# A graph attention kernel: candidate lists by quarters, and two VectorE products moved to ScalarE

## The chip, the cores and the metric

The kernel runs on one core of a Trainium2 chip. A core has five engines with a queue each, worked off in order: TensorE (PE in the profile, with its weight loads as PEld), VectorE (DVE), ScalarE (ACT), GpSimd (POOL) and SyncE (SP). They share an on-chip memory of 128 partitions (SBUF), an accumulator memory that TensorE writes (PSUM), and 16 DMA engines. The metric is the device time of one execution, from the first to the last instruction with what lies around it. A difference below 0.2% can't be told from none here.

## The reference

Two layers over one adjacency matrix `adj` of 3327 x 3327, of which about 2% of the entries are not zero (some 64 a row, and the diagonal). Layer 0 is graph attention with four heads, layer 1 a normalised graph convolution:

```python
h = jnp.maximum(_layernorm(x, axis=-1), 0.0)
# per head:
x1 = h @ w1;  x2 = h @ w2
E = jax.nn.leaky_relu(x1[:, None, :] + x2[None, :, :], negative_slope=0.01)
s = jnp.tanh((E @ a) / 8.0) * 8.0
s = jnp.exp(s) * adj
s = s / jnp.sum(s, axis=-1, keepdims=True)
out = leaky_relu(s @ h @ Wlin.T, 0.01)
x = x + jnp.concatenate(heads, axis=-1) @ w
# layer 1
h = jnp.maximum(_layernorm(x, axis=-1), 0.0)
A_t = adj + eye(n);  D_inv = A_t.sum(axis=1) ** -0.5
x = x + relu((D_inv[:, None] * A_t * D_inv[None, :]) @ (h @ W.T + b))
```

Only the entries of `adj` that are not zero matter to the scores. The kernel finds them, fetches the rows that they name, and computes the scores of those pairs alone.

## The kernel before

The nodes are padded to 3328 and worked in 26 blocks of 128 rows, each block in two halves of 64 rows. Each node has a row of 776 numbers in a table in device memory (its features, its scores' share, its four projected vectors, and its column of the adjacency matrix for one block); the tables of even and odd blocks alternate.

**Preparation of a block (`prep`).** It is a generator: it yields between small steps, and the steps of the blocks to come are put between the work of the current one. It does the following, in order:

- It turns the 128 x 3328 rows of `adj` into codes, a number for each column that is not zero (L410, L416, L418).
- It searches the codes for the entries: each row is cut into 64 segments of 52 columns, and one `max` (L422) writes the eight largest codes of a segment into `cand`. There the eight ranks of 32 segments lie together. Four ranks are kept as they are; the other four ranks of a half of the row are boiled down to a list of eight (L425).
- Between these searches it transposes the block on TensorE (L365), copies it out on ScalarE (L367) and stores it to device memory through ScalarE's DMA queue (L370). `known_step` uses the same copies for sums of layer 1 (L379, L385).
- ScalarE sums the rows (L443), and `load` fetches the rows of the next block through SP.
- `select` (L453, L456) takes the entries out of the candidates, eight a round, in 13 rounds: a `max` and a `match_replace` that strikes out what was found. The first four rounds go over one half of the candidates each (136 values), in turns; the other nine go over all (272). The first eight rounds give 64 slots a row; the last five give up to 40 further entries a row, the extra edges.
- `lq` spreads the 64 slots (L463, a product with the mask `modsel` on VectorE), TensorE turns them into another order (L470), and L473 makes the row numbers `idx` for the gathers.
- The extra edges of all rows are packed into lists of at most 256 a half block (L481 to L546), and the vectors of the block's own rows are projected (L551 to L568).

**Gathers.** GpSimd fetches the named rows with indirect DMAs of 128 rows each (L595): for a half block 32 of them into `g`, in four groups (w = 0 to 3) of eight, and two for the extra edges into `ge`. `g` has four buffers, `ge` has one. A group's buffer comes free when the last matrix product that reads it (L706 for `g`, L724 for `ge`) has been issued and done.

**Scores (`stage_z`, `stage_r`, `finish`).** For a part of a group, TensorE transposes the gathered vectors into `z` (L622, L625, L627; two buffers in PSUM), VectorE takes the maximum with minus the own vector (L638; L633, and ScalarE's L635, for the extra edges), and TensorE multiplies with the vector a (L657). `finish` closes a group: ScalarE copies the scores out (`ssb`, L666), TensorE transposes them (L675), VectorE adds the rows' shares (L678, L681), ScalarE takes tanh and exp (L686, L688), VectorE multiplies the weights with the adjacency entries (`wt`, L697), and TensorE sums the rows (L706). For the extra edges `am` picks an entry (L713) and `wo` is its product with the four heads' weights (L715), three tiles a half block, and L724 sums. `close` ends a block (L735 to L797).

**What sets the order.** The order is written by hand. `slot` is called 108 times a block, at fixed places between TensorE's instructions; in each it takes one step of every open `close` and `finish`, then as many steps of the preparations as are due (72 a block), then it issues gathers for which a buffer has been given back, and table loads (`weights`, on SP). A yield in `prep` or `finish` thus puts the rest one step later. Each engine then works its queue off in this order, and waits where what it needs isn't there.

**Layer 1** runs at the end (`layer1`): strips of the transposed matrix come in through SP's and ScalarE's DMA queues (L898) into the same `g` buffers, and TensorE multiplies (L988). Part of its sums is made earlier (`begin`, L924).

Last, a check of the lists: if a row had an entry that no list holds, a dense path would run in place of the result.

Of the kernel before, what the change touches and what calls it, by code (L numbers as in the profile page):

```python
# [9 lines left out]
F32 = mybir.dt.float32  # L10
AF = mybir.ActivationFunctionType
OP = mybir.AluOpType
# [3 lines left out]
P = 128  # L16
SLOPE = 0.01
CAP = 8.0
# [213 lines left out]
def _sparse_layers(tc, nc, x, adj, w1, w2, a, wlin, w, gw, gb, gb_sb, gwT, x_sb, dinv, flag, ident, out):  # L232
# [14 lines left out]
    H = w1.shape[0]  # L247
# [5 lines left out]
    WT = 8  # L253
# [3 lines left out]
    with ExitStack() as l0:  # L257
# [19 lines left out]
        modsel = res.tile([P, P], F32, name="modsel")  # L277
# [8 lines left out]
        pb = l0.enter_context(tc.tile_pool(name="pb", bufs=2))  # L286
# [66 lines left out]
        def prep(b, k):  # L353
# [38 lines left out]
                known[:] = [f for f in known if next(f, "end") != "end"]  # L392


            SOME = 8 + 4 * 32
            cand = pb.tile([P, 2, SOME + 4 * 32], F32, name="cand", bufs=1)
            tab_at = 0
            while b == 0 and tab_at < NB:
                tables_step(tab_at)
# [5 lines left out]
            for sgm in range(64):  # L405
                if sgm % 32 == 0:
                    codes = pa.tile([P, 2, part], mybir.dt.uint16, name="codes")
                    for i in range(2):
                        c0 = (sgm // 16 + i) * part
                        nc.vector.scalar_tensor_tensor(codes[:, i], adjb[:, c0:c0 + part], 0.0, code[:, c0:c0 + part],  # L410
                                                       op0=OP.not_equal, op1=OP.mult, accum_out=csum[:, sgm // 16 + i:sgm // 16 + i + 1])
                        lo, hi = max(c0, b * P), min(c0 + part, (b + 1) * P)
                        if lo < hi:
                            diag = pb.tile([P, P], F32, name="lq", bufs=1)[:, :hi - lo]
                            mine = codes[:, i, lo - c0:hi - c0]
                            nc.vector.scalar_tensor_tensor(diag, mine, -1.0, ident[:, lo - b * P:hi - b * P], op0=OP.mult, op1=OP.mult,  # L416
                                                           accum_out=csum[:, sums[0]:sums[0] + 1])
                            nc.vector.tensor_tensor(mine, mine, diag, OP.add)  # L418
                            sums[0] += 1
                        yield  # L420
                c = sgm // 32
                nc.vector.max(cand[:, c, 8:].rearrange("p (r s) -> p r s", s=32)[:, :, sgm % 32],  # L422
                              codes.rearrange("p a b -> p (a b)")[:, sgm % 32 * SEG:(sgm % 32 + 1) * SEG])
                if sgm % 32 == 31:
                    nc.vector.max(cand[:, c, :8], cand[:, c, SOME:])  # L425
                if sgm % 4 == 3:
                    yield
                    known_on()
                if sgm % 8 == 5 and tab_at < NB:
                    tables_step(tab_at)  # L430
                    tab_at += 4
# [14 lines left out]
            lists = pb.tile([P, 64 + 51], F32, name="lists")  # L446
            k.lists = lists
            flat = cand[:, :, :SOME]

            def select(r):  # L450
                top = lists[:, 8 * r:8 * r + 8]
                of = cand[:, r % 2, :SOME] if r < 4 else flat
                nc.vector.max(top, of)  # L453
                yield
                if 8 * r + 8 < 2 * SLOTS + EXTRA:
                    nc.vector.match_replace(out=of, in_to_replace=top, in_values=of, imm_value=0.0)  # L456
                yield

            for r in range(SLOTS // 4):
                yield from select(r)  # L460

            lq = pb.tile([P, 4, 8, 16], F32, name="lq", bufs=1)
            nc.vector.tensor_tensor(lq, modsel.rearrange("p (q s) -> p q s", q=8)[:, None].to_broadcast([P, 4, 8, 16]),  # L463
                                    lists[:, :64].rearrange("p (c s) -> p c s", c=4)[:, :, None, :].to_broadcast([P, 4, 8, 16]), OP.mult)
            yield
            yield
            yield
            pm = bank()
            for c in range(4):
# [191 lines left out]
        def finish(k, hb, w):  # L661
            g, s = k.g.pop((hb, w)), k.s
# [19 lines left out]
                                 k.ex[:, OVT * hb:OVT * hb + OVT, 42:42 + H])  # L682
            yield
            yield
            th = pb.tile([P, WT, H], F32, name="th")
            nc.scalar.activation(th[:, :nt], sc[:, :nt], AF.Tanh, scale=1.0 / CAP)  # L686
            pe = pb.tile([P, WT, H], F32, name="pe")
            nc.scalar.activation(pe[:, :nt], th[:, :nt], AF.Exp, scale=CAP)  # L688
            yield
            yield  # L690

# [20 lines left out]
            for t in range(OVT):  # L712
                nc.vector.scalar_tensor_tensor(am[:, t, :], code[:, :HALF], k.ex[:, OVT * hb + t, 41:42], g[:, t, BODY * hb:BODY * hb + HALF],  # L713
                                               op0=OP.is_equal, op1=OP.mult)
                nc.vector.tensor_tensor(wo[:, t], pe[:, t, None, :, None].to_broadcast([P, 8, H, 8]),  # L715
                                        am[:, t].rearrange("p (g q) -> p g q", q=8)[:, :, None, :].to_broadcast([P, 8, H, 8]), OP.mult)
                yield
            yield
            yield
# [83 lines left out]
        for b in range(NB):  # L803
            k = Blk()
            k.f0 = FEAT, 0
            k.g, k.b, k.ready, k.turned, k.closed = {}, b, False, False, False
            blks.append(k)
        NCODE = 20
        NLIST = 42
        NPREP = 72  # L810
# [553 lines left out]
```

## Time and profile before

| | |
|---|---|
| median of 6 runs | 2501.72 us (2496.91 to 2506.87) |
| the profiled execution | 2504.95 us, its span 2503.2 us |
| mean granted TensorE clock | 0.976 of full speed |
| DMA | 826.94 MB, 330 GB/s over the span; queue of the gathers 70.6% of the 16 engines' span, SP's 18.4%, ScalarE's 7.5% |
| first and last gather issued | 69.7 and 2375.3 us |
| 900 to 1200 us | busy: PE 277.6, DVE 265.6, ACT 84.9, POOL 225.7 us of 300; DMA share 0.99 |
| costliest groups | gathers L595 1614.0 us on POOL; L638 1010.0 us on DVE; L622 933.9 us on PE |
| segment searches L422 | 217.1 us, 1664 of 204 ns |

Times in the timelines are us from the span's start. In a timeline line the first number is the start, the second the length, then engine, line of the code, operation, what is written and read, how many instructions are taken together, and in brackets how long the engine stood idle before it and what ended that. In a line of the groups the count is followed by the busy time in us and the mean of one in ns, then by the idle time before. In a line of the waits the numbers are the sum in us, the number of waits and the longest. In the table by stretch each engine's busy time in the stretch is followed by its number of instructions, then the granted clock of TensorE, the DMA engines' busy share and the rate. A wait is put down to what released it last.

### The profile page before, as it was taken

To read this page: it belongs to the slowest core of one execution; us is meant where nothing else is said; L and a number is where in the kernel's file an instruction comes from. 1 tells how busy PE (TensorE), PEld (TensorE's weight loads), DVE (VectorE), ACT (ScalarE), POOL (GpSimd) and SP (SyncE) were. 2 spreads that over 40 slices of the span, in tenths; PEclk is the share of its full clock that TensorE was granted. 3 is DMA by queue.
4 is the path that set the end of the run, shared out by engine and by line. 5 is a ranking of instruction groups with operands and counts; after the bars stand their busy time and mean duration, and the time that the engine had idled before them with its cause. 6 is when DMAs were issued, how large, how long until landed. Compare 5 with 4: busy or idle time off the path is not lost.

```text
span 2503.2 us, 52385 instructions
## 1 busy us (share of the span) xinstructions
PE 2256.7 (90%) x19410; PEld 1595.7 (64%) x19410; DVE 2063.9 (82%) x6426; ACT 681.8 (27%) x1703; POOL 1737.0 (69%) x1822
## 2 busy tenths in 40 slices
PE   6589989999988998999999999999999999999978
PEld 4466666666666666666666666666676666666643
DVE  7588988888898889889888888988988898896623
ACT  4122232223223222322322232232232223222100
POOL 3477777777777777777777777777777777777700
PEclk8799999999999999999999999999999999999989
DMA  9999999999999999999999999999999999999985
GB/s 290 380 350 330 349 330 321 351 350 313 331 365 330 318 351 350 319 333 358 330 321 348 341 316 334 346 314 334 353 327 322 347 350 317 329 331 350 362 263 160
DMA packets 417844, 826.94 MB, mean 330 GB/s; under 512 B 38435, under 2 KB 288815, under 8 KB 414255
## 3 DMA queue, kind: packets, MB, share of 16 engines
q0 software_dynamic: 141440, 619.41, 70.6%
q1 hardware_dynamic: 165343, 147.87, 18.4%
q10 hardware_dynamic: 110800, 56.25, 7.5%
q8 instruction: 156, 2.56, 0.4%
q14 instruction: 105, 0.86, 0.1%
HBM read 754.47 MB, written 113.22 MB: 347 GB/s over the span
## 4 chain that ended last, share of the span: by engine, by line
PE 37%; DVE 25%; DMA 19%; POOL 11%; issue 6%; ACT 1%; SPq 0%; DVEq 0%; ACTq 0%; POOLq 0%
DMA g<-table,idx 14%; DVE r L638 14%; PE z L622 12%; POOL g L595 11%; PE s L657 10%; DVE cand L422 3%; PE ag L706 2%; PE z L627 2%; DMA g<-AT_d 2%; DVE codes L410 1%; DVE cand L456 1%; PE z L988 1%; DVE lists L453 1%; PE tr L924 1%; PE tr L675 1%
## 5 line engine op out<-in xcount | busy, mean ns | idle before, releaser
L595 POOL DMA_INDIRECT g<-table,idx x1664 | 1614.0, 970 | 586.0 <-issue 420.2
L638 DVE TENSOR_TENSOR r<-z,x1n 128x1024 f32<-128x1024 f32 x832 | 1010.0, 1214 | 129.8 <-PE z L622 127.1
L622 PE MATMUL z<-ident,g 128*128 128x128 f32 x6656 | 933.9, 279 | 102.0 <-DVE r L638 88.3
L622 PEld LDWEIGHTS z<-ident,g 128*128 128x128 f32 x6656 | 754.6, 143 | 263.7 <-DVE r L638 136.8
L657 PE MATMUL s<-r,sel 128*2 128x512 f32 (+1 forms) x3744 | 497.4, 585 | 8.8 <-DVE r L638 4.0
L666 ACT COPY ssb<-s 128x512 f32<-128x512 f32 x260 | 146.8, 565 | 499.6 <-PE s L657 498.8
L657 PEld LDWEIGHTS s<-r,sel 128*2 128x2 f32 x3744 | 79.9, 84 | 250.9 <-issue 188.8
L422 DVE MAX8 cand<-codes 128x8 f32<-128x52 uint16 x1664 | 217.1, 204 | 0.0
L686 ACT ACTIVATE th<-sc 128x32 f32<-128x32 f32 x260 | 58.4, 225 | 438.9 <-DVE sc L681 413.1
L706 PEld LDWEIGHTS ag<-g,wt 128*32 128x32 f32 x3328 | 99.3, 110 | 89.8 <-issue 79.9
L367 ACT COPY at<-tr 128x512 f32<-128x512 f32 (+1 forms) x175 | 97.2, 556 | 212.6 <-PE tr L365 190.8
L675 PE MATMUL tr<-ident,ssb 128*128 128x128 f32 x988 | 150.8, 273 | 2.8 <-ACT ssb L666 2.7
L633 DVE TENSOR_TENSOR r<-z,x1n 128x128 f32<-128x128 f32 x104 | 30.0, 289 | 138.6 <-PE z L627 136.0
L706 PE MATMUL ag<-g,wt 128*32 128x133 f32 x3328 | 140.3, 281 | 0.0
L453 DVE MAX8 lists<-cand 128x8 f32<-128x272 f32 (+1 forms) x338 | 133.2, 394 | 2.2
L365 PE MATMUL tr<-ident,adjb 128*128 128x128 f32 x676 | 109.2, 285 | 24.8 <-DMA adjb<-in_adj_dram 13.0
L635 ACT ACTIVATE r<-z 128x512 f32<-128x512 f32 x104 | 62.2, 598 | 247.2 <-DVE r L633 241.1
L627 PE MATMUL z<-oi,x1b 128*128 128x256 f32 x416 | 125.1, 383 | 0.0
L675 PEld LDWEIGHTS tr<-ident,ssb 128*128 128x128 f32 x988 | 118.1, 141 | 9.7 <-ACT ssb L666 3.4
L595 POOL DMA_INDIRECT ge<-table,idxo x104 | 99.9, 960 | 32.5 <-issue 15.1
L456 DVE MATCH_REPLACE8 cand<-lists,cand 128x272 f32<-128x272 f32 (+1 forms) x312 | 118.0, 378 | 0.0
L410 DVE SCALAR_TENSOR_TENSOR codes<-adjb,code 128x832 uint16<-128x832 f32 x104 | 105.3, 1015 | 13.6 <-DMA adjb<-in_adj_dram 13.6
(199 smaller groups left out, 2410.0 us busy)
## 6 DMA issues: line engine op xcount, KB each, us to landing
adjb<-in_adj_dram SPq DMA_DIRECT2D x26, 1664.0 KB
table<-AT_d SPq DMA_DIRECT2D x26, 1664.0 KB
AT_d<-at ACTq DMA_DIRECT2D x150, 256.0 KB
g<-table,idx POOLq DMA_INDIRECT x1664
table<-img SPq DMA_DIRECT2D x12, 1296.0 KB
adjb<-AT_d SPq DMA_DIRECT2D x72, 128.0 KB
g<-AT_d ACTq DMA_DIRECT2D x25, 256.0 KB
g<-AT_d SPq DMA_DIRECT2D x25, 256.0 KB
```

The costliest lines, as they stand in the source:

```text
L410: nc.vector.scalar_tensor_tensor(codes[:, i], adjb[:, c0:c0 + part], 0.0, code[:, c0:c0 + part], op0=OP.not_equal, op1=OP.mult, accum_out= ...
L422: nc.vector.max(cand[:, c, 8:].rearrange("p (r s) -> p r s", s=32)[:, :, sgm % 32], codes.rearrange("p a b -> p (a b)")[:, sgm % 32 * SEG: ...
L453: nc.vector.max(top, of)
L456: nc.vector.match_replace(out=of, in_to_replace=top, in_values=of, imm_value=0.0)
L595: return nc.gpsimd.indirect_dma_start(out=g[:, t, lo:hi], out_offset=None, in_=tab, in_offset=bass.IndirectOffsetOnAxis(ap=at[:, t:t + 1], ...
L622: nc.tensor.matmul(z[:, i, q * P:(q + 1) * P], g[:, m % 2 * 4 + q, c0:c0 + D], ident, is_transpose=True, start=(q == 0 or m < 8), stop=(m ...
L627: nc.tensor.matmul(z[:, i, :n], k.x1b[:, h * D:(h + 1) * D], k.oi[:, hb * n:(hb + 1) * n], start=False, stop=True, skip_group_check=True)
L638: nc.vector.tensor_tensor(r.rearrange("p h (i s) -> p h i s", s=16), z.rearrange("p h (i s) -> p h i s", s=16), k.x1n[:, 2 * hp:2 * hp + 2 ...
L657: nc.tensor.matmul(k.s[32 * h:32 * h + 2, :n], sel[:, h, 31 - at:33 - at], r[h // 2][:, h % 2, :n], start=(at == 0), stop=(at == 1 or m == 8))
L666: nc.scalar.copy(ssb[:, :nk * P], s[:, :nk * P])
L675: nc.tensor.transpose(pt[:, q, :], ssb[:, q * P:(q + 1) * P], ident)
L706: nc.tensor.matmul(ag[32 * cg:32 * cg + 32, u, :WORK], wt[:, t].rearrange("p h q -> p (h q)"), g[:, t, f0:f0 + WORK], start=(w == 0 and t ...
```

## The change

- The candidates are kept by quarters of the row (16 segments each) in place of halves: three ranks of each segment as they are, and a list of eight from the other five ranks of the quarter (80 values). Two quarters side by side hold 112 candidates, all four 224.
- Of the 13 rounds of `select` the first six, in place of four, go over one half of the row.
- `lq` is made by eight ScalarE activations (a copy with a factor for each row), four in a step and four in the next, in place of one VectorE product. The number of steps stays the same.
- `wo` is made by four ScalarE activations a tile, one for each head, in place of one VectorE product.
- tanh writes over its input; the tile `th` is gone.

```diff
--- before.py
+++ after.py
@@ -392,8 +392,8 @@
                 known[:] = [f for f in known if next(f, "end") != "end"]
 
 
-            SOME = 8 + 4 * 32
-            cand = pb.tile([P, 2, SOME + 4 * 32], F32, name="cand", bufs=1)
+            SOME = 8 + RANKS * 16
+            cand = pb.tile([P, 4, 8 + 8 * 16], F32, name="cand", bufs=1)
             tab_at = 0
             while b == 0 and tab_at < NB:
                 tables_step(tab_at)
@@ -418,10 +418,10 @@
                             nc.vector.tensor_tensor(mine, mine, diag, OP.add)
                             sums[0] += 1
                         yield
-                c = sgm // 32
-                nc.vector.max(cand[:, c, 8:].rearrange("p (r s) -> p r s", s=32)[:, :, sgm % 32],
+                c = sgm // 16
+                nc.vector.max(cand[:, c, 8:].rearrange("p (r s) -> p r s", s=16)[:, :, sgm % 16],
                               codes.rearrange("p a b -> p (a b)")[:, sgm % 32 * SEG:(sgm % 32 + 1) * SEG])
-                if sgm % 32 == 31:
+                if sgm % 16 == 15:
                     nc.vector.max(cand[:, c, :8], cand[:, c, SOME:])
                 if sgm % 4 == 3:
                     yield
@@ -449,7 +449,7 @@
 
             def select(r):
                 top = lists[:, 8 * r:8 * r + 8]
-                of = cand[:, r % 2, :SOME] if r < 4 else flat
+                of = cand[:, r % 2 * 2:r % 2 * 2 + 2, :SOME] if r < 6 else flat
                 nc.vector.max(top, of)
                 yield
                 if 8 * r + 8 < 2 * SLOTS + EXTRA:
@@ -460,10 +460,10 @@
                 yield from select(r)
 
             lq = pb.tile([P, 4, 8, 16], F32, name="lq", bufs=1)
-            nc.vector.tensor_tensor(lq, modsel.rearrange("p (q s) -> p q s", q=8)[:, None].to_broadcast([P, 4, 8, 16]),
-                                    lists[:, :64].rearrange("p (c s) -> p c s", c=4)[:, :, None, :].to_broadcast([P, 4, 8, 16]), OP.mult)
-            yield
-            yield
+            for q in range(8):
+                nc.scalar.activation(lq[:, :, q], lists[:, :64].rearrange("p (c s) -> p c s", c=4), AF.Copy, scale=modsel[:, 16 * q:16 * q + 1])
+                if q % 4 == 3:
+                    yield
             yield
             pm = bank()
             for c in range(4):
@@ -682,10 +682,9 @@
                                  k.ex[:, OVT * hb:OVT * hb + OVT, 42:42 + H])
             yield
             yield
-            th = pb.tile([P, WT, H], F32, name="th")
-            nc.scalar.activation(th[:, :nt], sc[:, :nt], AF.Tanh, scale=1.0 / CAP)
+            nc.scalar.activation(sc[:, :nt], sc[:, :nt], AF.Tanh, scale=1.0 / CAP)
             pe = pb.tile([P, WT, H], F32, name="pe")
-            nc.scalar.activation(pe[:, :nt], th[:, :nt], AF.Exp, scale=CAP)
+            nc.scalar.activation(pe[:, :nt], sc[:, :nt], AF.Exp, scale=CAP)
             yield
             yield
 
@@ -712,8 +711,8 @@
             for t in range(OVT):
                 nc.vector.scalar_tensor_tensor(am[:, t, :], code[:, :HALF], k.ex[:, OVT * hb + t, 41:42], g[:, t, BODY * hb:BODY * hb + HALF],
                                                op0=OP.is_equal, op1=OP.mult)
-                nc.vector.tensor_tensor(wo[:, t], pe[:, t, None, :, None].to_broadcast([P, 8, H, 8]),
-                                        am[:, t].rearrange("p (g q) -> p g q", q=8)[:, :, None, :].to_broadcast([P, 8, H, 8]), OP.mult)
+                for h in range(H):
+                    nc.scalar.activation(wo[:, t, :, h], am[:, t].rearrange("p (g q) -> p g q", q=8), AF.Copy, scale=pe[:, t, h:h + 1])
                 yield
             yield
             yield
@@ -805,6 +804,7 @@
             k.f0 = FEAT, 0
             k.g, k.b, k.ready, k.turned, k.closed = {}, b, False, False, False
             blks.append(k)
+        RANKS = 3
         NCODE = 20
         NLIST = 42
         NPREP = 72
```

## The prediction

> **What bounds the kernel now.** The page's first part comes first: no engine is full, and four resources lie close together. So the next view is busy time by stretch, here over one block (one block is 128 rows, 26 in all) in the middle of the run.
>
> ```profile
> PE 2256.7 (90%) x19410; PEld 1595.7 (64%) x19410; DVE 2063.9 (82%) x6426; ACT 681.8 (27%) x1703; POOL 1737.0 (69%) x1822
> ```
>
> ```profile
> core 0: us, PE busy (x) PEld busy (x) DVE busy (x) ACT busy (x) POOL busy (x), PEclk, DMA share, GB/s
> 1231.00:1265.00 34.00, 31.24 (x285) 22.65 (x284) 30.42 (x83) 9.12 (x21) 25.55 (x27) 1.00 1.02 375
> 1265.00:1297.00 32.00, 30.91 (x280) 22.11 (x278) 24.76 (x70) 9.79 (x30) 24.63 (x25) 1.00 0.93 295
> 1297.00:1320.00 23.00, 20.10 (x178) 14.39 (x177) 22.12 (x90) 6.59 (x16) 15.78 (x17) 0.93 1.00 326
> ```
>
> In the last stretch VectorE is busy 22.12 of 23 us and TensorE is not; in the middle one it is TensorE (30.91 of 32). The DMA engines are full in the outer two. POOL's 25.55 of 34 hides that it hardly pauses by choice: its timeline shows a gather of 0.95 us and a standing pause of 0.30, one after the other.
>
> ```profile
> 1316.47 0.94 POOL L595 DMA_INDIRECT ge<-table,idxo  x1 [0.30 <-PE z L622]
> 1319.80 0.94 POOL L595 DMA_INDIRECT g<-table,idx  x1 [2.39 <-PE ag L706]
> 1321.05 0.94 POOL L595 DMA_INDIRECT g<-table,idx  x1 [0.30 <-issue]
> ```
>
> A block has 68 gathers, so POOL alone needs 68 x 1.25 = 85.1 us. The same gather of the block before starts at 1231.24, so this block took 88.56. The rest is mainly one wait, always at the first gather of a block, for TensorE to be through with a buffer (L706). The waits of POOL between 264 and 2205 us (22 blocks) give its sum:
>
> ```profile
> POOL g L595 <- PE ag L706: 38.2, 25, 3.2
> ```
>
> Less 0.30 of standing pause each, 25 waits hold 38.2 - 7.5 = 30.7 us, 1.23 apiece. So POOL and the consumers (TensorE and VectorE in turns) run at almost one pace, the consumers slower by about 1.4 us a block. A faster consumer can win those 30.7 us in the steady part before POOL binds alone; a slower one costs one for one.
>
> **The change, part by part.** The durations, by shape:
>
> ```profile
> L453 DVE MAX8 lists<-cand 128x8 f32<-128x272 f32 x234 | 102.7, 439 | 2.2
> L456 DVE MATCH_REPLACE8 cand<-lists,cand 128x272 f32<-128x272 f32 x208 | 88.5, 426 | 0.0
> L715 DVE TENSOR_TENSOR wo<-pe,am 128x256 f32<-128x256 f32 x156 | 67.0, 430 | 9.0
> L453 DVE MAX8 lists<-cand 128x8 f32<-128x136 f32 x104 | 30.5, 293 | 0.0
> L456 DVE MATCH_REPLACE8 cand<-lists,cand 128x136 f32<-128x136 f32 x104 | 29.5, 283 | 0.0
> L456 DVE MATCH_VALUE_LOAD cand<-lists,cand 128x8 f32 x312 | 27.3, 88 | 5.6
> L463 DVE TENSOR_TENSOR lq<-modsel,lists 128x512 f32<-128x512 f32 x26 | 17.8, 684 | 0.0
> L425 DVE MAX8 cand<-cand 128x8 f32<-128x128 f32 x52 | 15.4, 295 | 1.8
> ```
>
> *Selection.* Now 4 half rounds (136 values) and 9 full ones (272, the last without replacement): 4 x 664 + 9 x 439 + 8 x 514 = 10.72 us a block. After: 6 half rounds of 112 and 7 full ones of 224. The two measured widths put a line through each operation (1.07 and 1.05 ns a value), so 267 and 258 ns at 112, 388 and 376 at 224: 6 x 613 + 7 x 388 + 6 x 464 = 9.18. Gain 1.5. Bounds: no shorter at all for the narrower width, 0.6 (two long rounds become short ones); the 224 as cheap as 136, 2.8. I take the line, since 112 and 224 lie close to its points.
>
> *List of eight* (L425): 4 x 80 values for 2 x 128: 4 x 233 - 2 x 295 = +0.3 by the same line; between +0.2 (the 52-wide row, 204) and +0.6 (unshortened). The 64 segment searches only write at another stride: 0; their 204 ns could rise, by no row here.
>
> *Row spread (lq) and extra edges' weights (wo).* VectorE loses 684 + 6 x 430 = 3.3 us a block. VectorE in all: -1.5 + 0.3 - 3.3 = -4.5 us a block, some -116 of its 2064.
>
> ScalarE gains 8 + 24 small operations a block, 128x64 with a per-row scale. No such form is in the trace. Nearest: two L740 (128x128, per-row scale) take 0.63 us together where one takes 0.363, so the second adds 0.27; with 64 columns fewer at 0.83 ns (256 columns 373 ns, 512 586 ns) 0.21. The source is SBUF here, as in L779/L780, which follow each other by 0.31, so 0.26. I take 0.25; ends 0.10 (the four 128x4 copies L490 to L493 follow by 0.09) and 0.40 (L779 alone, no overlap). That is 832 x 0.25 = 208 us on an engine that is idle for 1821.
>
> The Trainium skill speaks against such a move: "ScalarE: Activation LUTs", Rules for kernel authors, sends multiplications to VectorE. Its cost section (What ACT_TABLE_LOAD costs) gives 186 ns + 0.833 a column + 93 per pointer operand, less 93 of overlap; an estimate from it is 0.24 us each, 1.9 us for the eight, and the sum below would stay.
>
> What is queued behind them matters more. Round lq, in the timelines of VectorE, TensorE and ScalarE:
>
> ```profile
> 1252.57 0.68 DVE L463 TENSOR_TENSOR lq<-modsel,lists 128x512 f32<-128x512 f32 x1
> 1253.33 1.04 PE L470 MATMUL tr<-tmask,lq 128*128 128x16 f32 x8
> 1251.77 0.48 ACT L666 COPY ssb<-s 128x384 f32<-128x384 f32 x1 [0.61 <-PE s L657]
> 1261.12 1.53 PE L724 MATMUL ag<-ge,wo 128*128 128x133 f32 x12
> 1260.30 0.59 ACT L666 COPY ssb<-s 128x512 f32<-128x512 f32 x1 [4.81 <-PE s L657]
> ```
>
> TensorE reaches L470 as lq is ready (1253.25). After the change the eight start behind ssb, at 1252.25, and end at about 1254.3: TensorE, whose queue is in order, stands 1.0 us there (0 by 0.10 each, 2.1 by 0.40), and everything behind it, z first, is late by that. For wo there is room: each group of four waits for its am; the last am (end near 1259.4) comes some 0.7 us earlier without the wo between, so its four end near 1259.8, as VectorE's did (1259.83), ahead of ssb (1260.30) and of L724. In a block's other half L724 comes over 1.6 us after wo, and the at copies between move by at most a group, 1 us. The at copies' AT_d stores, issued from ScalarE's queue, move with them; SP's load of the table behind the last of them (1320.7) feeds gathers from about 1408 on. The gathers, SP's loads and every yield stay in place; tanh in place removes a buffer and no work, and sc has a second buffer: 0.
>
> *On the path.* Of VectorE's 4.5 us I let half count, 2.2: the path changes between the two engines about evenly, as the stretches show. Less the stand of 1.0, the consumers gain 1.2 us a block. A wait of POOL can shrink by no more than its own length: the 25 waits, each cut by 1.2 or to nothing, give about 22 of the 30.7.
>
> *Start.* lq now queues behind the 3 us row sum (L443, until 63.5) and ends near 65.5 instead of 58.95; idx moves from 62.5 to about 69, still just ahead of the first gather (69.7), which waits for table stores. What would be late is covered by VectorE's wait of 13.6 us for the next rows (to 88.75) and POOL's waits at 84 and 106. Without that cover it would cost 6.6. *End.* From the last gather (2375) TensorE and the strip loads set the pace; the last wo (2413) go ahead of the strip loads in ScalarE's queue: 0.
>
> **The sum.** The profiled execution took 2504.95 (span 2503.2), 3.2 above the median of 2501.7. 2505 - 22 = 2483, so 2480 on the median's footing; own range 2468 to 2492.
>
> **The rivals.** *Nothing gained.* The DMA share is 1.00 and 1.02 in the stretches where the wait lies; gathers issued earlier would then only land as late as now. Against: the stretch between has 0.93, so 2.2 us are free there. All but a couple of us lost: 2500.
>
> *All of it.* All waits go (-30.7), and with fewer holes the half clock too. From 1314 to 1318 the granted clock is 0.61, and L657 x16 takes 2.98 us there instead of 1.83 to 1.90, in the very path to the awaited buffer. The PEclk 0.93 above is this one dip; 11 such dips lie in the steady part, about 1 us each, together -11: 2505 - 42 - 3 = 2460. "TensorE: Matmul & The Clock Gate" (Rules) of the skill asks only that no idle gap exceed about 3 us; here the dip follows holes of 0.70 and 1.02 us, so the row decides and gives no such safety.
>
> *Slower: TensorE stands at L470.* At 0.40 us each the eight hold it 2.1 us a block. If only a quarter of VectorE's relief (1.1) reaches the path, the consumers are 1.0 slower in each of 26 blocks: 2502 + 26 = 2528. It decides from the point where the stand exceeds the relief on the path, 2.2 by my share. For it: L470 has no slack at all now. Against: ScalarE's own rows overlap.
>
> **How the numbers follow.** Forecast 0.47, nothing 0.18, all 0.19, slower 0.16. The range 2456 to 2512 leaves out the outer part of the last two. A measurement can tell about 0.2% (5 us) from no change. Faster: the forecast, all, and a little of nothing, 0.68; same 0.14; slower 0.18.
>
> **What would show it.** VectorE busy near 1950 and ScalarE near 890; L453 near 267 and 388 ns; the wait of POOL for L706 near 9 us above its pauses instead of 30.7; TensorE waiting about 1 us a block for lq at L470. Wrong if that wait of POOL grows, if ScalarE's 64-column operations follow each other by 0.4 us, or if TensorE stands before L724 or for ssb.

## The result, and the profile after

The changed kernel takes 2518.84 us (median of 20 runs, 2513.86 to 2537.81) against 2501.56 us for the kernel before (45 runs, 2493.41 to 2511.55). The ratio is 1.0088, 95% interval 1.0074 to 1.0101: slower by 0.9% by this ratio, and by 17 us (0.7%) from median to median. Forecast were 2480 us, range 2456 to 2512. The 20 runs fall into groups, 11 at 2513.9 to 2519.2 us with a mean granted TensorE clock of 0.973 to 0.976, six at 2531.6 to 2537.8 with 0.965 to 0.968 and three between, which no run here explains, so that a figure against this median is good to some 5 us (their mean is 2523.4). The profiled execution took 2516.6 us, 2.2 below the median; its span is 2514.9.

Line numbers from L686 on are one lower in the changed kernel than before (L705 for L706, L712 for L713, L723 for L724; L715 is `wo` in both), and the kernels of the experiments have shifts of their own: L470 is L471 and L595 is L596 where a selection round was put ahead of it. The text below calls a wait of TensorE at L470 for `lq` the stand at L470.

First the page's engine line of the kernel after:

```profile
PE 2225.1 (88%) x19410; PEld 1594.4 (63%) x19410; DVE 1961.8 (78%) x6296; ACT 880.7 (35%) x2535; POOL 1736.9 (69%) x1822
```

VectorE lost 102 us and ScalarE gained 199, nearly as forecast (VectorE near 1950, ScalarE near 890 us busy). The work went where it should; the time did not follow. Next the groups by shape, to hold against the durations in the prediction:

```profile
L453 DVE MAX8 lists<-cand 128x8 f32<-128x224 f32 x182 | 70.9, 390 | 2.0
L456 DVE MATCH_REPLACE8 cand<-lists,cand 128x224 f32<-128x224 f32 x156 | 58.5, 375 | 0.0
L453 DVE MAX8 lists<-cand 128x8 f32<-128x112 f32 x156 | 41.9, 269 | 0.0
L456 DVE MATCH_REPLACE8 cand<-lists,cand 128x112 f32<-128x112 f32 x156 | 40.4, 259 | 0.0
L425 DVE MAX8 cand<-cand 128x8 f32<-128x80 f32 x104 | 25.5, 245 | 3.6
L715 ACT ACTIVATE wo<-am,pe 128x64 f32<-128x64 f32 x624 | 157.5, 335 | 134.6 <-DVE am L712 124.3 <-DVE r L638 9.8 <-ACT at L367 0.4
L464 ACT ACTIVATE lq<-lists,modsel 128x64 f32<-128x64 f32 x208 | 52.6, 338 | 5.1 <-DVE lists L453 5.1
```

Every duration came out close to what was worked out. ScalarE's small activations take 335 to 338 ns each but overlap: 157.5/624 = 0.252 us and 52.6/208 = 0.253 us of engine time. New is the idle time of ScalarE *before* its `wo`: 124.3 us spent waiting for VectorE's `am` (L712) with the next work queued behind. Who pays for that stands in the waits of TensorE over the whole run, kernel after:

```profile
PE z L622 <- DVE r L638: 107.1, 141, 1.7
PE tr L379 <- ACT at L367: 37.2, 18, 2.2
PE tr L379 <- DVE sc L678: 29.3, 22, 2.2
PE tr L470 <- ACT lq L464: 23.9, 26, 5.8
```

and the same rows of the kernel before:

```profile
PE z L622 <- DVE r L638: 114.7, 147, 3.1
PE tr L379 <- DVE sc L678: 29.4, 22, 2.2
PE tr L379 <- ACT at L367: 4.3, 18, 0.2
```

Two things are new in what TensorE waits for on ScalarE: 24 us at L470 for `lq`, where before it had no such wait, and 33 us more at L379 for `at`, the copy of the transposed tile. The timeline of ScalarE and TensorE, kernel after, shows the second one:

```profile
1208.38 1.06 ACT L715 ACTIVATE wo<-am,pe 128x64 f32<-128x64 f32 x4 [2.30 <-DVE am L712]
1209.35 0.24 ACT L383 COPY part<-tr 128x128 f32<-128x128 f32 x1
1209.49 0.58 ACT L367 COPY at<-tr 128x512 f32<-128x512 f32 x1
1207.37 0.60 PE L622 MATMUL z<-ident,g 128*128 128x128 f32 x4
1210.12 1.93 PE L379 MATMUL tr<-at,x_sb 128*128 128x128 f32 x8 [2.15 <-ACT at L367]
1211.85 1.06 PE L622 MATMUL z<-ident,g 128*128 128x128 f32 x4
```

The first group of `wo` reaches the head of ScalarE's queue at 1206.1 and waits 2.30 us for `am`, which on VectorE stands behind a maximum of 1.21 us (L638) and four searches (L422, 0.55 us). The copies L383 and L367 stand behind `wo`, though their own input is there: TensorE ended the transposes for L367 near 1207.5. TensorE works its queue off in order as well: L379 waits 2.15 us for `at`, with `z` behind it, and VectorE then waits for `z` (L638 for L622: 190.6 us in the whole run, 127.1 before). In the kernel before, the same L379 waits 0.24 us. The product that waits is the second of a block (`known_step` with j0 = 4). It exists only from the preparation of the ninth block on, when enough blocks are closed: 18 blocks, 18 waits, the first at 679 us.

The pace shows it. From the first gather of a block to that of the next one (blocks counted from 0), the kernel before takes 87.99 us a block in blocks 2 to 8 and 88.34 in blocks 9 to 23. The kernel after takes 86.80 and 89.43: faster by 1.2 us a block, as forecast, in the first of these, and slower by 1.1 once the waits at L379 have set in. POOL's wait at the first gather of a block tells the same: in blocks 3 to 8 of the kernel after it is the standing pause of 0.30 us alone, so the gathers set the pace there, and in blocks 10 to 24 it is 1.6 to 4.8 us in all but one. (These are single profiled executions.) The stretches of one block of the kernel after (cut at the same distances from its first gather as those of before):

```profile
core 0: us, PE busy (x) PEld busy (x) DVE busy (x) ACT busy (x) POOL busy (x), PEclk, DMA share, GB/s
1138.60:1172.60 34.00, 30.32 (x286) 22.36 (x284) 29.42 (x90) 14.38 (x41) 25.74 (x28) 1.00 1.00 359
1172.60:1204.60 32.00, 31.14 (x293) 22.24 (x292) 24.68 (x71) 9.71 (x28) 24.38 (x26) 1.00 0.95 317
1204.60:1228.20 23.60, 19.03 (x157) 15.02 (x158) 19.41 (x78) 9.00 (x27) 15.78 (x16) 0.93 1.00 324
```

In the last stretch VectorE was busy 22.12 of 23 us before; now 19.41 of 23.6, and TensorE 19.03: neither is full; the timeline above shows one place where they wait for each other by way of ScalarE. And the waits of POOL between 263 and 2212 us, whose sum the forecast wanted near 9 us above its pauses:

```profile
POOL g L595 <- PE ag L705: 39.8, 18, 4.8
```

39.8 - 18 x 0.30 = 34.4 us instead of 30.7 before: the wait grew, which the prediction had named as a sign of being wrong.

### The profile page after: what moved, and what is told of

Its sections match the earlier page's. It is cut to its first block, busy times and chain, and to the rows that moved or that the text cites. A ratio compares the mean times of both kernels' runs of the same rounds, so it can differ in the third digit from the quotient of the medians.

```text
span 2514.9 us, 53085 instructions
## 1 busy us (share of the span) xinstructions
PE 2225.1 (88%) x19410; PEld 1594.4 (63%) x19410; DVE 1961.8 (78%) x6296; ACT 880.7 (35%) x2535; POOL 1736.9 (69%) x1822
## 4 chain that ended last, share of the span: by engine, by line
PE 42%; DVE 25%; DMA 15%; POOL 8%; issue 5%; ACT 3%; SPq 1%; ACTq 0%; DVEq 0%; POOLq 0%
DVE r L638 14%; PE z L622 14%; PE s L657 11%; DMA g<-table,idx 9%; POOL g L595 8%; DVE cand L422 3%; PE z L627 3%; PE ag L705 2%; DMA adjb<-AT_d 2%; PE tr L379 1%; DVE codes L410 1%; DMA g<-AT_d 1%; DMA table<-img 1%; PE tr L675 1%; PE z L988 1%
## 5 line engine op out<-in xcount | busy, mean ns | idle before, releaser
L595 POOL DMA_INDIRECT g<-table,idx x1664 | 1612.7, 969 | 591.7 <-issue 420.5
L638 DVE TENSOR_TENSOR r<-z,x1n 128x1024 f32<-128x1024 f32 x832 | 1011.0, 1215 | 191.5 <-PE z L622 190.6
L622 PE MATMUL z<-ident,g 128*128 128x128 f32 x6656 | 929.3, 279 | 96.6 <-DVE r L638 83.1
L622 PEld LDWEIGHTS z<-ident,g 128*128 128x128 f32 x6656 | 755.4, 143 | 252.0 <-DVE r L638 122.8
L657 PE MATMUL s<-r,sel 128*2 128x512 f32 (+1 forms) x3744 | 468.9, 585 | 8.7 <-DVE r L638 4.4
L422 DVE MAX8 cand<-codes 128x8 f32<-128x52 uint16 x1664 | 217.6, 204 | 0.0
L715 ACT ACTIVATE wo<-am,pe 128x64 f32<-128x64 f32 x624 | 157.5, 335 | 134.6 <-DVE am L712 124.3
L685 ACT ACTIVATE sc<-sc 128x32 f32<-128x32 f32 x260 | 58.4, 225 | 347.0 <-DVE sc L681 325.6
L705 PEld LDWEIGHTS ag<-g,wt 128*32 128x32 f32 x3328 | 98.5, 110 | 91.3 <-issue 84.8
L367 ACT COPY at<-tr 128x512 f32<-128x512 f32 (+1 forms) x175 | 96.6, 552 | 149.0 <-PE tr L365 123.1
L705 PE MATMUL ag<-g,wt 128*32 128x133 f32 x3328 | 140.2, 281 | 0.0
L379 PE MATMUL tr<-at,x_sb 128*128 128x128 f32 x488 | 72.7, 289 | 69.3 <-ACT at L367 37.2
L595 POOL DMA_INDIRECT ge<-table,idxo x104 | 100.9, 971 | 32.7 <-issue 9.4
L379 PEld LDWEIGHTS tr<-at,x_sb 128*128 128x128 f32 x488 | 60.6, 193 | 92.8 <-issue 47.1
```

The lines of the kernel that those rows point to most:

```text
L379: nc.tensor.matmul(pq[:, :P], x_sb[:, j0 + q, :], at[:, q, :], start=(q == 0), stop=(q == js[-1]))
L595: return nc.gpsimd.indirect_dma_start(out=g[:, t, lo:hi], out_offset=None, in_=tab, in_offset=bass.IndirectOffsetOnAxis(ap=at[:, t:t + 1], ...
L622: nc.tensor.matmul(z[:, i, q * P:(q + 1) * P], g[:, m % 2 * 4 + q, c0:c0 + D], ident, is_transpose=True, start=(q == 0 or m < 8), stop=(m ...
L638: nc.vector.tensor_tensor(r.rearrange("p h (i s) -> p h i s", s=16), z.rearrange("p h (i s) -> p h i s", s=16), k.x1n[:, 2 * hp:2 * hp + 2 ...
L657: nc.tensor.matmul(k.s[32 * h:32 * h + 2, :n], sel[:, h, 31 - at:33 - at], r[h // 2][:, h % 2, :n], start=(at == 0), stop=(at == 1 or m == 8))
L705: nc.tensor.matmul(ag[32 * cg:32 * cg + 32, u, :WORK], wt[:, t].rearrange("p h q -> p (h q)"), g[:, t, f0:f0 + WORK], start=(w == 0 and t ...
```

## The experiments

All times are medians; in brackets the ratio to the kernel before with its 95% interval. Theory A: the loss is the copy `at` held behind `wo` in ScalarE's queue. Theory B: it is the stand at L470 for `lq`. Theory C: it is the work added to ScalarE, wherever it is put.

### Undoing one move at a time

**e1_wo_dve**: `wo` back on VectorE, the rest of the change kept.

```
-                for h in range(H):
-                    nc.scalar.activation(wo[:, t, :, h], am[:, t]..., AF.Copy, scale=pe[:, t, h:h + 1])
+                nc.vector.tensor_tensor(wo[:, t], pe..., am[:, t]..., OP.mult)
```

> The extra edges' weights (wo) go back to VectorE as before the change; the row spread (lq) stays on ScalarE. Theory A (order in ScalarE's queue): in the changed kernel the copy of a turned tile (at, L367) stands in ScalarE's queue behind wo, which waits for VectorE's am; TensorE then waits at L379, 37.2 us in 18 waits, and half clock follows those holes. Then that wait falls to about 4.3 us as before the change, and the time by 37 - 4 = 33 us and some us of half clock, less half of VectorE's 6 x 0.43 - 6 x 0 = 2.6 us a block given back (26 x 1.3 = 34): so the two nearly cancel if VectorE is half of the path, and the time lies between 2485 and 2520; the blocks from the ninth on become as even with the first eight as they were before the change. Theory B (TensorE's stand of 23.9 us at L470 for lq is the loss): nothing is regained, the stand stays 24 us, and the time rises by VectorE's share to 2530 or more. Theory C (the added load of ScalarE itself, 157 us of wo and 53 of lq): three quarters of the loss of 17 us go, 2506.

Measured: 2525.93 us (1.0096, 1.0072 to 1.0120). The waits of TensorE in e1:

```profile
PE tr L470 <- ACT lq L464: 23.9, 26, 5.8
PE tr L379 <- ACT at L367: 4.3, 18, 0.2
```

The wait at L379 is gone and the blocks are even again (88.77 us in blocks 2 to 8, 88.87 after), both as A said, but at the slow pace; the time lies between the ranges of A (2485 to 2520) and B (2530 or more). So `wo` early on ScalarE, with its 33 us of waiting, still comes out 7 us ahead of `wo` on VectorE; what makes e1 slow is something else.

**e2_lq_dve**: `lq` back on VectorE (the eight activations replaced by the one `tensor_tensor` and its two yields).

> The row spread (lq) goes back to VectorE as before the change; the extra edges' weights (wo) stay on ScalarE. Theory A (the turned tile's copy is held behind wo in ScalarE's queue): the wait of TensorE at L379 for that copy stays near 37 us, the stand at L470 (23.9 us) goes, VectorE gets 26 x 0.68 = 18 us back of which half counts: 2519 - 24 + 9 = about 2504 to 2519, still not under the kernel before. Theory B (the stand at L470 is the loss): the whole 24 us are regained, 2495. Theory C (ScalarE's load): a quarter of the loss, 2515.

Measured: 2500.88 us (0.9998, 0.9984 to 1.0012). The stand at L470 is gone but for 0.7 us, the wait at L379 stays (37.4 us), and 17.9 us are regained, which is the whole loss; the time lies between what B (2495) and A (2504 to 2519) said.

**e3_sel_only**: both back on VectorE.

> Both lq and wo go back to VectorE: what is left of the change is the lists in quarters, the six half rounds, the list of eight and tanh in place. All theories: the stand at L470 and the long wait at L379 are gone. VectorE is 1.2 us a block shorter than before the change; if half of that is on the path the time is 2502 - 26 x 0.6 = 2486, with POOL's wait for L705 near 20 us above its pauses; if none, 2502. If it is slower than 2507, the loss lies in the selection and not in what moved to ScalarE, and theories A and B are both wrong.

Measured: 2501.70 us (1.0005, 0.9987 to 1.0023). The quarters, with VectorE at 2033.6 us instead of 2063.9, change nothing in the median, where half of the relief would have given 2486. The four kernels together:

| | `wo` on VectorE | `wo` on ScalarE, early |
|---|---|---|
| `lq` on VectorE | 2501.7 (e3) | 2500.9 (e2) |
| `lq` on ScalarE | 2525.9 (e1) | 2518.8 (the change) |

`lq` on ScalarE costs 24.2 and 17.9 us; `wo` on ScalarE, early, gains 0.8 and 7.1. Counted from e3, which has neither move, the loss comes in with `lq`, which brings the stand at L470 (B). `wo` takes 2.6 us a block from VectorE and still wins next to nothing; whether A's wait is the reason, the next two runs test.

### The order in ScalarE's queue

**e4_wo_late**: the changed kernel, each group of `wo` issued two steps after its `am`; its reader L723 stays in its step.

```
+            def spread(t):
+                for h in range(H):
+                    nc.scalar.activation(wo[:, t, :, h], ...)
             for t in range(OVT):
                 nc.vector.scalar_tensor_tensor(am[:, t, :], ...)
-                for h in range(H):
-                    nc.scalar.activation(wo[:, t, :, h], ...)
+                if t == 2:
+                    spread(0)
                 yield
+            spread(1)
             yield
+            spread(2)
             yield
```

> wo stays on ScalarE, but each group of four is issued two steps after its am instead of right behind it, so that it need not wait for VectorE at the head of ScalarE's queue; the work and its consumer's place (L723) are the same. Theory A (order in the queue): TensorE's wait at L379 for the turned tile's copy falls from 37.2 us to below 10, half clock with it, and with VectorE's relief kept the time falls by some 30 to 40 us to 2480 to 2490, under the kernel before. Theory B (stand at L470): unchanged, 2519. Theory C (ScalarE's load): unchanged, 2519. A third way: the last group now ends too late for L723, TensorE waits there instead (up to 1 us a half block, 52 us), and the time stays or rises.

Measured: 2481.30 us (0.9916, 0.9895 to 0.9936), 37.5 us under the changed kernel with the same work on every engine. The waits of TensorE and the timeline of ScalarE and TensorE in e4:

```profile
PE tr L470 <- ACT lq L464: 22.4, 25, 5.8
PE tr L379 <- ACT at L367: 4.3, 18, 0.2
```

```profile
1198.72 0.59 ACT L367 COPY at<-tr 128x512 f32<-128x512 f32 x1 [0.61 <-PE tr L365]
1199.34 0.37 ACTq L370 DMA_DIRECT2D AT_d<-at  x1
1199.75 2.02 ACT L713 ACTIVATE wo<-am,pe 128x64 f32<-128x64 f32 x8 [0.44 <-DVE am L716]
1199.36 1.16 PE L379 MATMUL tr<-at,x_sb 128*128 128x128 f32 x8 [0.24 <-ACT at L367]
```

The copy now goes ahead of `wo`, and L379 waits 0.24 us. A is shown: same load, other order, the wait gone and the time with it. C is out, since ScalarE's load is the same (883.6 us). The stores of the copies (L370) move with them, but are no rival: POOL waits for a table twice in the whole run, both times before 106 us, 37.8 us in the changed kernel and 38.3 in e4. One new wait for `wo` is the price in e4, 4.6 us, once, at 2403 us, after the last gather.

**e12_wo_one**: one step after its `am` instead of two.

> The changed kernel with wo one step after its am instead of two (e4: 2481.3) or none (2518.8): the dose of theory A. TensorE's wait at L379 for the turned tile's copy was 37.2 us with none and 4.3 with two. If it is the place in ScalarE's queue that counts, wait and time move together: a wait of x us gives about 2481 + (x - 4). I expect 5 to 15 us of wait and 2482 to 2492; if one step is enough, 4 and 2481. If the time moved without the wait, theory A would be wrong.

Measured: 2479.07 us (0.9909, 0.9895 to 0.9924), the wait for `at` at 4.3 us. One step is enough; it gives no partial dose (5 to 15 us of wait had been expected).

### The stand at L470

**e7_lq_late**: the changed kernel with the product of `lq` and the index arithmetic two steps later; one selection round (`select(SLOTS // 4)`) is moved ahead of it.

```
             yield
+            yield from select(SLOTS // 4)
             pm = bank()
...
-            for r in range(SLOTS // 4, SLOTS // 4 + EXTRA // 8):
+            for r in range(SLOTS // 4 + 1, SLOTS // 4 + EXTRA // 8):
```

> The changed kernel with only the product of lq (L470) two steps later; wo in its early place. TensorE's stand at L470 falls from 23.9 us to a few; the wait at L379 for the turned tile's copy stays near 37 us. By e2 (lq on VectorE, 2500.9) the time is 2495 to 2501. If it stays at 2519, the stand was a symptom and lq's work itself is what costs.

Measured: 2496.98 us (0.9980, 0.9968 to 0.9991): 21.9 us regained. Of the stand one wait is left; the wait at L379 is unchanged:

```profile
PE tr L471 <- ACT lq L464: 4.6, 1, 4.6
PE tr L379 <- ACT at L367: 37.2, 18, 2.2
```

The work stayed on ScalarE and 23.9 - 4.6 = 19.3 us of standing went: the stand was the price, paid about one for one. Where it is paid shows in the pace: in blocks 9 to 23 the changed kernel takes 89.43 us a block, e7 88.48 and e2 88.67; in blocks 2 to 8, where the gathers set the pace, it takes 86.80 against 87.23 and 87.35, so the stand cost nothing there.

**e6_both_late** (both edits) and **e5_wo_late_lq_dve** (`wo` late, `lq` back on VectorE):

> Both stay on ScalarE; wo two steps late as in e4, and TensorE's product of lq (L470, with the index arithmetic behind it) two steps later too, one more selection round lying before it. The stand at L470 (22.4 us in e4) should fall to a few us, most of it the first block's. Against e4: 2481 - 18 = about 2463 if the stand is what costs; VectorE keeps its relief, so not slower than e5. Rival: idx comes some 2 us later in every block, which costs nothing in the steady part if the gathers are far behind it, and up to 4 us at the start. If the stand goes and the time stays at 2481, POOL or the DMA engines bind.

> wo on ScalarE two steps late as in e4 (2481.3), and the row spread (lq) back on VectorE. So far lq on ScalarE cost 2518.8 - 2500.9 = 17.9 us with wo early on ScalarE, and 2525.9 - 2501.7 = 24.2 with wo on VectorE, against 22 to 24 us of standing at L470. If the stand is paid in full whatever wo does: 2481 - 18 to 24 = 2457 to 2463. Rival (POOL's floor): in e4 POOL's wait for L705 is down to 15.3 us in 12 waits, 15.3 - 12 x 0.30 = 11.7 above its pauses, so the consumers are no longer the bound in most blocks and no more than about 12 us, and a few at the start, can be won: 2465 to 2470. Rival (VectorE): the 0.68 us a block given back to VectorE eats most of it: 2475 to 2481.

Measured: e6 2474.86 us (0.9882, 0.9860 to 0.9904), e5 2477.17 us (0.9906, 0.9879 to 0.9933). With `wo` late, taking the stand away wins only 4 to 6 us (the runs of e5 and e6 scatter by about as much), not 18 to 24, although TensorE still stood 22.4 us there in e4; both times lie above the 2457 to 2463 of a stand paid in full. e5 falls into the range of the rival on VectorE (2475 to 2481). But e6 gives VectorE nothing back and is only 2.3 us below e5, so that is not what eats the gain. What shows is POOL's floor: POOL's wait for L705, 45.2 us over the whole of the changed kernel, is 15.3 in e4, so little was left to win, and 7.1 in e5 and 1.5 in e6. The 2465 to 2470 that went with that rival were not reached.

### The moves without the quarters

**e8_before_wo_late**: the kernel before with `wo` late on ScalarE and nothing else. **e9_before_both_late**: with `lq` on ScalarE too, its product two steps later.

> The kernel before with one edit alone: wo on ScalarE, each group two steps after its am; the lists in halves, four ranks, lq on VectorE, tanh in its own buffer. It differs from e5 by the selection alone. e3 put the selection at nothing (2501.7 against 2502.1), though VectorE is 30 us shorter there. If a cut of VectorE only counts where nothing else binds, and the selection is again worth nothing, this equals e5 within 5 us; if the selection's 1.2 us a block counts half once wo is away, this is 15 us above e5. Against the kernel before, with 2.6 us a block less on VectorE: half on the path is 2502 - 34 = 2468; POOL's floor puts it near 2470 as well; if VectorE's relief counts for nothing, 2502.

> The kernel before with both moves and neither half of the selection's change: wo two steps after its am (as in e8, 2470.7), lq on ScalarE with its product (L470) two steps later (as in e6). VectorE loses another 0.68 us a block against e8. If VectorE is still half of the path: 2470.7 - 26 x 0.34 = 2462. If POOL's pace binds (in e8 no wait of POOL for L706 is left among the longest): 2467 to 2472. If the later idx costs at the start: up to 2475.

Measured: e8 2470.70 us (0.9873, 0.9850 to 0.9896), e9 2463.24 us (0.9856, 0.9839 to 0.9873). Both lie below the kernels with quarters above; e8 had been expected within 5 us of e5 or 15 above it, and is 6.5 below. The waits of e9, of POOL and then of TensorE:

```profile
POOL g L596 <- PE ag L707: 0.3, 1, 0.3
```

```profile
PE z L623 <- DMA g<-table,idx: 22.7, 29, 3.9
PE tr L471 <- ACT lq L464: 4.6, 1, 4.6
PE tr L379 <- ACT at L367: 4.3, 18, 0.2
```

In e9 the wait of POOL for TensorE's last reader (L706 before, L707 here) is down to 0.3 us, and a block takes 86.43 us against the 85.1 of 68 gathers at 1.25; it is now TensorE that waits for gathered rows (22.7 us, 8.7 before).

### What VectorE's time is worth

**e10_before_sel_longer**: the kernel before, with three selection maxima a block issued twice.

```
                 nc.vector.max(top, of)
+                if r in (4, 5, 9):
+                    nc.vector.max(top, of)
                 yield
```

> The kernel before, with three of the nine full selection maxima of each block issued twice (rounds 4, 5 and 9: VectorE +3 x 0.44 = 1.3 us a block, +34 us in all), the opposite of what the selection's change does (-1.2). e3 showed that the shorter selection gains nothing. If the selection lies where TensorE or another wait ends last anyway, this costs nothing as well: 2502 within 4. If half of VectorE's time there is on the path, as the prediction took it, 2502 + 17 = 2519, and then something in the quarters must give back what their shorter rounds win. If all of it is on the path, 2536.

Measured: 2518.11 us (1.0055, 1.0040 to 1.0071). VectorE's busy time rose by 34.9 us, the time by 16.7: 0.48. From the other side e8 took 60.4 us from VectorE (2003.5 against 2063.9) and 30.9 from the time: 0.51. The half that the prediction took is measured twice, by medians; the intervals leave 0.29 to 0.51 and 0.43 to 0.62. But then the selection's 30 us should have given 15 in e3, and gave none.

### Where the selection's gain went

**e11_before_wo_late_quarters** is e8 with the selection of the change and tanh in a buffer of its own.

> e8 (wo two steps late, 2470.7) with the lists in quarters and the six half rounds, but tanh still in a buffer of its own: e5 (2477.2) without tanh in place. If tanh in place costs, this is at 2470; if the quarters cost 6 us, at 2477; if the two differed by chance, in between, and the selection is worth nothing here as in e3.

Measured: 2476.85 us (0.9899, 0.9885 to 0.9913), the same as e5: tanh in place does nothing, and the selection by quarters costs 6 us on e8, where less VectorE time had been expected to win or to do nothing. The next four take the selection apart on the base of e9: **e13_quarters_layout** (quarters, but four ranks and four half rounds), **e14_quarters_three_ranks** (e13 with three ranks), **e15_selection_whole** (e14 with six half rounds) and **e16_six_half_rounds** (halves and four ranks, only the rounds):

```
-                of = cand[:, r % 2, :SOME] if r < 4 else flat
+                of = cand[:, r % 2, :SOME] if r < 6 else flat
```

> e9 (both moves, late; 2463.2) with the lists laid out in quarters, four maxima L425 of 64 values instead of two of 128, but still four ranks and four half rounds. VectorE by the widths: L425 +0.27, rounds of 144 and 288 instead of 136 and 272 +0.36: +0.63 us a block, 16 us in all. If the layout itself (the shorter stride of L422's results, the two more maxima among the row steps) is what gives time back, 2463 + 8 + 10 = 2475 to 2485; if only VectorE's time counts, by half, 2471; if POOL's pace covers it, 2463.

> e13 with three ranks instead of four: rounds of 112 and 224 values, still four half rounds. VectorE against e9 -0.68 us a block (-18 in all), against e13 -1.3 (-34). If the layout is what costs, this stands some 17 under e13 and still above e9; if the ranks (other entries in the lists, so other rows in the gathers) are what costs, e13 is at e9's time and this is 5 to 12 above it.

> e14 with six half rounds: the whole selection of the change upon e9, tanh in its own buffer (e6, 2474.9, without tanh in place). VectorE -31 us against e9. By e6 2470 to 2475 again. If it is at 2463 or below, e6 differed by chance or by tanh in place.

> e9 with only the number of half rounds changed, six of 136 values and seven of 272: VectorE -0.58 us a block, -15 in all; layout and ranks as before. If the half rounds are what costs (the lists then hold the entries in another order), 2468 to 2475; if not, 2455 to 2463.

| on the base of e9 (2463.2) | VectorE busy | time (ratio to before) |
|---|---|---|
| e13, layout in quarters | +16 us | 2471.44 (0.9880, 0.9861 to 0.9899) |
| e14, and three ranks | -17 us | 2474.40 (0.9885, 0.9867 to 0.9903) |
| e15, and six half rounds | -28 us | 2473.61 (0.9890, 0.9874 to 0.9906) |
| e16, six half rounds alone | -15 us | 2462.36 (0.9836, 0.9821 to 0.9852) |

The order of the entries that six half rounds give costs nothing (e16). On this base less work on VectorE wins nothing any more (e16; e15 against e13), which fits a pace set by the gathers. What appears with the quarters and stays is about 8 to 11 us. In e13 half of its 16 us more of VectorE would explain that; in e14 and e15, where VectorE is shorter than in e9, it can't, so the layout, or the three ranks in these two, has a price of its own (e14 came out as neither of its two expectations had it). It is not the searches themselves: L422 takes 204 ns in halves and in quarters. Part of it is in the tail: from the last gather to the end the kernels with halves (before, e8, e9, e10, e16) take 126.9 to 128.1 us, those with quarters 128.1 to 134.0. In e3's profile the tail is 4.6 us longer than in that of before and a block 0.43 us faster (9.5 us in 22 blocks, of which 7 may be chance: that execution lies 3.6 below its median, the one of before 3.4 above). ScalarE's DMA queue, which carries the strips, takes 7.8% of the engines' span in e13 to e15 and 7.5% before, but 7.7% in e9 too, so that settles nothing. By what the quarters cost time stays open.

## Why the prediction was wrong

**What bounds it: right.** POOL's pace of 1.25 us a gather is the floor and the 30.7 us of POOL's wait were there to be won: the kernel before with both moves in a better order (e9) wins them, at 2463, near the rival "all of it" (2460). (Of the 25 waits a few, 0.3 to 0.8 us each, lie elsewhere than at a block's first gather, against the "always"; nothing hangs on it.)

**Durations: right.** Selection 9.2 us a block as worked out (269, 259, 390, 375 ns for a forecast of 267, 258, 388, 376), L425 245 ns, ScalarE 0.25 us an operation. The estimate from the figures of the Trainium skill, "ScalarE: Activation LUTs" (What ACT_TABLE_LOAD costs), 0.24 us, agrees with 157.5/624 = 0.252.

**The failed step: "For wo there is room ... the at copies between move by at most a group, 1 us."** The step asked when `wo` would be ready for its reader L724 and found it in time, which it was: no wait of L723 for `wo` shows. It looked at the copies behind `wo` as if they were delayed by ScalarE's *work*, four times 0.25 us. They were delayed by the *wait* at the head of the queue, 2.30 us for `am`, and TensorE had a reader of the copy (L379) right there: 37.2 us in place of 4.3. e4 puts a price of 37.5 us on it, and gives 2481.3, the forecast of 2480. That e4 lies so near is in part luck: it has the selection by quarters, whose 1.2 us a block were counted in and gave nothing (e3).

**L470: the stand was right, its price wrong.** Forecast 1.0 us a block, measured (23.9 - 5.8)/25 = 0.72 and 5.8 in the first block. The prediction set it against the relief of all parts together. e7 shows that it is paid about one for one (19.3 us of standing, 21.9 of time); e1 against e3 gives 24.2 us net of what `lq` takes from VectorE, 0.68 us a block, which is worth half at best. The rival "slower: TensorE stands at L470" named the place; its condition, 0.40 us an operation, did not hold and was not needed. With the relief of `wo` eaten at L379, a stand below the forecast size was enough. Either mended alone ends the loss (e4 2481, e7 2497), so it took both.

**Half of VectorE's relief on the path: right as a rate** (0.48 in e10, 0.51 in e8), **wrong for the selection's part**, which gave nothing (e3). Of the terms put at nothing, the segment searches held (204 ns, as before); "*End.*", 0, did not: from the last gather to the end the changed kernel takes 133.4 us, 127.9 before.

**Start: right against the profile of before**, with the first gather at 70.1 us (69.7 before) and block 2 at 263.2 (263.9). The other kernels have their first gather at 69.0 to 70.6 where L470 follows `lq` on ScalarE at once (e1, e4, e12) and at 66.4 to 68.7 elsewhere, so 2 to 3 us may be lost there after all; with one profile each this isn't settled.

**Half clock: not the cause of the difference between the two profiled executions.** Between 263 and 2170 us both have 11 stretches at half clock.

## What to carry to other kernels

Work moved to an idle engine that works its queue off in order is to be priced by what its first instruction *waits for*, and not only by what it takes: list what is queued behind it on that engine and who, on the bounding engine, reads that. If its input comes late, issue it a step later, behind the short copies that feed others; here one step was worth 40 us (e12) at no cost in work. In this kernel a wait of TensorE counted about one for one while TensorE and VectorE set the pace (e7), whereas time taken from VectorE, which shares the path, counted half (e8, e10), so a product that saves VectorE 0.68 us and makes TensorE stand for 0.72 loses.

## What the runs showed of the hardware

- Eight or twelve equal 128x64 activations follow each other by 0.24 to 0.25 us on ScalarE though each takes 0.335 us (2.02 us for eight, 2.97 for twelve).
- Holes of TensorE well under 3 us are followed by half clock. After the 2.15 us at L379 above, eight products take 1.93 us instead of 1.13 to 1.16, and four transposes 1.06 instead of 0.60. The granted clock was 0.50 for 3.41 us. In the profile of after it follows 7 of the 16 holes of 2.15 us. The part "Why this matters for your kernels" of "TensorE: Matmul & The Clock Gate" in the Trainium skill (the prediction calls it "Rules") speaks of gaps above some 3 us; these runs show shorter ones that do it.
- Which holes do it goes by where they fall. Every change of the granted clock lies on one grid of 3.413 us. Of the 48 holes of 2.15 to 2.23 us at L379 in after, e2 and e7, half clock follows all 20 that have 1.97 us or more in one cell of the grid, and none of the 28 with 1.94 or less. Summed over all holes of a cell, the kernel before (263 to 2170 us) shows 1.68 us or more of TensorE idle in each of the 11 cells ahead of half clock and 1.67 or less in every other; in after it is 1.80 or more ahead of half clock, and up to 1.94 elsewhere. The cell with the hole shown above, and the next one, kernel after:

```profile
core 0: us, PE busy (x) PEld busy (x) DVE busy (x) ACT busy (x) POOL busy (x), PEclk, DMA share, GB/s
1206.89:1210.31 3.41, 1.26 (x11) 1.02 (x10) 3.38 (x14) 1.69 (x6) 2.54 (x3) 1.00 0.99 343
1210.31:1213.72 3.41, 3.41 (x17) 3.41 (x17) 1.47 (x11) 2.02 (x8) 2.77 (x3) 0.50 0.96 297
```

- The two kernels that keep `wo` early and have no stand at L470 ran at a mean granted clock of 0.973 (e2) and 0.974 (e7), as medians of their runs, those with `wo` late or on VectorE at 0.975 to 0.979; single runs of the two kinds overlap (e3 goes down to 0.971). How much of the price of the wait at L379 is this clock was not taken apart.
- The price of a wait is not a constant: the stand at L470, set against `lq` on VectorE, cost 24.2 us with `wo` on VectorE, 17.9 with `wo` early, and 4 with `wo` late, when the gathers nearly set the pace.
